# Moving the zero halves, x's other halves, addresses and lists of places among the table chunks, with column copying from step 3

## The chip, the core and the metric

The kernel runs on one core of one Trainium2 chip. The metric is the device time of one execution, in microseconds. Before the change the median of three runs is 2145.4 us (2143.6 to 2152.13).

The core's engines are PE (matrix products), DVE and ACT (element-wise work on the 128-partition memory, products' results included), POOL (here: it issues the gathers) and SP (here: it issues transfers). Each runs its own instructions in the order in which they are written, and they meet by semaphores. Transfers that SP and ACT issue share eight landing counters; each transfer is given one of them, and it is not issued before the last transfer of that counter has landed.

## What is computed

One layer of message passing on a graph: 12,500 nodes of 64 numbers (x), 200,000 edges with 32 numbers each (edge_attr), each edge with a source and a destination; the edges are sorted by destination.

```python
def _mlp(x, W1, b1, W2, b2):
    return relu(x @ W1 + b1) @ W2 + b2
msg_in = concatenate([nodes[row], nodes[col], edge_features], axis=-1)   # 64 + 64 + 32
messages = _mlp(msg_in, mW1, mb1, mW2, mb2)                              # 160 -> 128 -> 64
aggregated = segment_sum(messages, col, num_segments=12500)
upd_in = concatenate([nodes, aggregated], axis=-1)
out = layernorm(nodes + _mlp(upd_in, uW1, ub1, uW2, ub2))                # 128 -> 128 -> 64
```

Here row is the source of an edge and col its destination.

## The kernel before

**Tiles and steps.** The edges are cut into 1563 tiles of 128. A step works on six tiles (SUB), a group on two steps (twelve tiles, SUP); there are 261 steps. The first matrix of the message MLP is split by its three inputs. A = x times its rows for the source and B = x times its rows for the destination plus the bias are tables of one row per node. The hidden row h of an edge is the relu of A[source] + B[destination] + its edge numbers times the last rows.

**One step.** PE makes "pc" for six tiles: L410 multiplies an operand l (one-hot places of the destinations in a window of 32 rows, and the edge numbers) with rhs (a window of B and the weights of the edge numbers). Then the A rows come in: POOL gathers them, one instruction for each tile of 128 edges (L239), into nine row buffers, and PE adds them by a product with the identity (L437). DVE makes h from it by a relu (L450). In the next step L490 sums h over the destinations. The operand l and the selection band of a later group are made on DVE (L273, L281). SP loads what l and rhs need (L257 the destinations, L294 the edge numbers, L318 the window of B).

**The first eight steps** do not gather rows of A but rows of x itself (48 gathers, 64 numbers a row), since the table is not there yet. PE transposes them (L326) into PSUM "pt", ACT copies that to xt (L327), PE multiplies xt with the weights w1a (L429), and ACT makes h (L431). Gathers from table A begin at step 8 and wait until the whole table is written.

**The table chunks.** Ahead of step 0 table A is made in 13 chunks of eight blocks of 128 nodes (the last has two). A chunk is 16 or fewer matmuls into PSUM "pb" (L646), a copy of one half on ACT (L656), a copy of the other on DVE (L654), and one write of 512 KB that ACT issues (L658). pb has two buffers, and the copies' tile "tb" has four. The loop stands at L738 to L762: behind chunk k it issues four of the x gathers on POOL, the first of which waits for the chunk's ACT copy (eight more were issued ahead of the loop). Behind chunk 2 comes the first piece of table B, behind chunks 5 and 7 the operands of groups 0 and 1, and behind chunk 10 offsets(), a run of small DVE instructions on one partition that makes the lists of places from the list of windows.

**Column copying.** Not every A row is gathered. x transposed lies in the on-chip memory as xtop and xbot: blocks of nodes alternate between the two, and where one holds a node's 64 numbers the other holds zeros. For a copied group, its last two tiles (of six in the step) are not gathered from A. Each of the 128 columns of a tile "xc" is made instead from one column of xtop and one of xbot: ACT adds them (L381), DVE joins their bits (L389), each after loading the columns' addresses from col_a into registers (L357). PE then multiplies xc with w1a (L413). progress(s) says how many groups are to be copied by the end of step s; PACE gives its slope, and a group is used three steps later. COPIED lists the steps that use one: 118 of them, the first in steps 16, 18, 20.

**What the first steps do besides.** rest(s) issues the preparations of column copying: others() loads the other halves of xtop and xbot on SP (L630, L631, L633) in steps 3, 5 and 7; zeros() writes the zero halves on ACT (L639), two instructions of 64 x 1568 in each of the steps 3 to 10; columns_list() loads the source numbers (L336) and makes col_a on DVE (L339) in step 9. relative(), in steps 1 to 3, loads the destinations (L599) and the windows (L600, into col_a as scratch space) and subtracts them on DVE (L601).

**The order** of each engine is that of the program text, loop by loop (manual scheduling). Where a step gathers for a later one, its gathers are spread behind PE's matmuls by an added dependency called "pace".

Of the kernel before, what the change touches and what calls it, by code (L numbers as in the profile page):

```python
# [17 lines left out]
P = 128  # L18
# [56 lines left out]
LEAD = 8  # L75
SBASE = (33556480, 33554432)
CBASE = 33566720
PACE = ((11, 0.48), (50, 0.505), (130, 0.483), (170, 0.469), (261, 0))
# [49 lines left out]
def gnn_kernel(ctx: ExitStack, tc: tile.TileContext, x1T, x, eT, e_rows, src, src_row, dst, dst_row, wlist, wrow, wnext, whalf,  # L128
# [117 lines left out]
    with tc.tile_pool(name="work", bufs=2) as work, tc.manual_schedule():  # L246
# [74 lines left out]
        def transpose(s):  # L321

            a = xg.pop(s)[1]
            xt = work.tile([P, SUB // 2, P], F32, name="xt", tag="tb", bufs=4)
# [270 lines left out]

        def relative(a, b):

            wbc = col_a.rearrange("p a e b -> p (a e b)")[:, :b - a]
            nc.sync.dma_start(dst_s[:, a:b], dst[:, a:b])  # L599
            nc.sync.dma_start(wbc, wrow[:, a:b].broadcast_to([P, b - a]))  # L600
            nc.vector.tensor_tensor(drc[:, a:b], dst_s[:, a:b], wbc, op=ALU.subtract)  # L601
# [67 lines left out]
        def offsets():  # L669
# [5 lines left out]
            while k < K:  # L675
# [11 lines left out]
                k += n  # L687
            nc.vector.tensor_tensor(ustep[:, 1:], usup[:, 1:], usup[:, :-1], op=ALU.subtract)
            for v in (woff[:, :NSUB * LS], ustep[:, 1:]):
                nc.vector.tensor_scalar(v, v, 0.0, float(UN), op0=ALU.max, op1=ALU.min)  # L690
            v = woff[:, :NSUB * LS]
            nc.vector.tensor_scalar(wcnt[:, :NSUB * LS], v, 4.0, float(CBASE), op0=ALU.mult, op1=ALU.add)
            nc.vector.tensor_scalar(v, v, 4.0, float(SBASE[0]), op0=ALU.mult, op1=ALU.add)
            for k, d, n in runs:
                if k % 2 == 0:
                    k, n = k + 1, n - 1
                if n > 0:
                    o = ov[:, UPD[k]:UPD[k] + n * d].rearrange("o (n d) t -> o n (d t)", n=n)[:, ::2]
                    nc.vector.tensor_scalar(o, o, float(SBASE[1] - SBASE[0]), None, op0=ALU.add)

# [34 lines left out]
        for r in rhs:  # L735
            for o in EK:
                nc.sync.dma_start(r[o:o + DE], mW1[2 * D:, :].unsqueeze(1).broadcast_to([DE, SUP // 2, DH]))
        for k, c in enumerate(range(0, NB, NCH)):  # L738
# [4 lines left out]
            if k == 2:  # L743
                chunk_b(0, [B0v, Bv])
            if k == 3:
# [15 lines left out]
            if k == 10:  # L761
                offsets()  # L762
        assert not first

        def rest(s):

            if 3 <= s < 9 and s % 2:
                others((s - 3) // 2 * 4, (s - 3) // 2 * 4 + 4)
            if 3 <= s < 11:
                zeros(s - 3, 8)  # L770
            if s == 6:
                first_nodes(8, NODES)
            if s == 9:
                columns_list()
# [361 lines left out]
```

## Time and profile before

| | before |
|---|---|
| median of three runs | 2145.4 us |
| the profiled execution | 2147.86 us |
| its span in the trace | 2146.1 us |
| gathers from x / from table A | 48 / 1279 |
| single columns on ACT / on DVE | 7872 / 7232 |
| first copy of a chunk on ACT (L656) | 12.49 us |
| last copy of a chunk on ACT | 80.54 us |
| h of steps 0, 1, 2, 3 (start of L431) | 83.6, 87.3, 99.7, 112.1 us |
| first gather from table A | 84.58 us |

Times within the execution count from the start of the span. In a row of the timeline stand the start, the duration, the engine, the line of the kernel, the operation, what it writes and reads, its shape, and in brackets how long the engine had been idle before it and what released it. "remote" is a release that no recorded end explains, and "issue" is a time in which the engine waited for nothing that the profile shows. In a group of instructions stand the busy time of all, the mean of one in nanoseconds, and behind the second bar the idle time before them with its most frequent releaser. A busy share is an average over the whole span, so a stage of some ten microseconds doesn't show in it; for these the timeline and the table of stretches are read.

### The profile page before, as it was taken

How to read it: one execution, taken by the hardware profiler on the slowest of the kernel's cores; microseconds unless marked ns; L12 is line 12 of the kernel's file. 1: busy time of each engine (PE TensorE's matmuls, PEld its weight loads, DVE VectorE, ACT ScalarE, POOL GpSimd, SP SyncE). 2: the span in 40 equal slices, each digit the busy share in tenths (PEclk: the TensorE clock that was granted, in tenths of full speed). 3: DMA queues.
4: the chain of work that ended last, by engine and by line, in shares of the span. 5: the costliest groups of instructions: out<-in, count | busy, mean ns of one | idle time of the engine just before them, and what ended most of it. 6: DMA issues, size and time to landing. Idle time of an engine off the chain costs nothing. (4 is left out here: it accounts for less than half of the span.)

```text
span 2146.1 us, 47795 instructions
## 1 busy us (share of the span) xinstructions
PE 1692.0 (79%) x10742; PEld 1284.5 (60%) x10742; DVE 1135.8 (53%) x8047; ACT 1575.1 (73%) x8029; POOL 1257.7 (59%) x1336
## 2 busy tenths in 40 slices
PE   3476877888778887878887887888887888888888
PEld 3454665666555665656565656556665666666666
DVE  2414555565555555565555645565555565555553
ACT  1155988769869697889677877787877877878872
POOL 6565666665666666555656655565656666666650
PEclk8667877777787778787877777787788787878788
DMA  8452333332222222232223323233333333333331
GB/s 221 114 138 73 104 89 97 89 92 74 78 74 78 75 79 79 76 85 78 76 81 83 89 75 88 81 94 83 81 89 85 84 96 85 92 86 94 85 89 40
DMA packets 207836, 190.41 MB, mean 89 GB/s; under 512 B 57909, under 2 KB 174093, under 8 KB 207549
## 3 DMA queue, kind: packets, MB, share of 16 engines
q0 software_dynamic: 42464, 85.48, 16.0%
q1 hardware_dynamic: 150396, 92.86, 15.5%
q10 hardware_dynamic: 14690, 8.99, 1.5%
q8 instruction: 90, 1.47, 0.3%
q14 instruction: 196, 1.61, 0.2%
HBM read 169.15 MB, written 18.02 MB: 87 GB/s over the span
## 5 line engine op out<-in xcount | busy, mean ns | idle before, releaser
L239 POOL DMA_INDIRECT xg<-tab_a,src_s x1279 | 1211.0, 947 | 806.7 <-issue 264.7
L381 ACT ACTIVATE xc<-xtop,xbot 128x1 f32 x7872 | 1491.8, 293 | 163.6 <-issue 118.8
L389 DVE TENSOR_TENSOR xc<-xtop,xbot 128x1 int32 x7232 | 607.0, 155 | 470.6 <-issue 455.4
L490 PE MATMUL sums<-band,h 128*128 128x96 f32 x3126 | 539.2, 327 | 144.0 <-issue 88.4
L490 PEld LDWEIGHTS sums<-band,h 128*128 128x128 f32 x3126 | 476.8, 233 | 174.3 <-issue 103.4
L437 PE MATMUL pc<-xg,band 128*128 128x384 f32 (+1 forms) x1008 | 451.5, 574 | 31.8 <-issue 26.7
L410 PE MATMUL pc<-rhs,l 64*128 64x128 f32 x3126 | 371.5, 351 | 89.7 <-issue 66.3
L410 PEld LDWEIGHTS pc<-rhs,l 64*128 64x128 f32 x3126 | 291.8, 234 | 140.5 <-issue 97.5
L450 DVE TENSOR_SCALAR h<-pc 128x768 f32<-128x768 f32 x252 | 240.3, 953 | 197.2 <-PE sums L490 69.5
L437 PEld LDWEIGHTS pc<-xg,band 128*128 128x128 f32 x1008 | 216.4, 237 | 148.8 <-issue 96.3
L273 DVE TENSOR_TENSOR l<-l,cps 128x768 f32<-128x768 int32 (+1 forms) x134 | 127.1, 948 | 146.0 <-PE pc L437 66.8
L486 PEld LDWEIGHTS <-one 128*1 128x1 bf16 x1563 | 56.5, 81 | 215.3 <-issue 211.0
L561 ACT ACTIVATE y<-cps 128x256 f32<-128x256 f32 (+1 forms) x36 | 13.7, 382 | 179.8 <-issue 86.9
L486 PE MATMUL cnt<-band,one 128*1 128x32 bf16 x1563 | 89.6, 180 | 42.2 <-issue 40.9
L544 ACT ACTIVATE hTu<-sums,ub_s 128x416 f32<-128x416 f32 (+1 forms) x36 | 21.7, 603 | 96.0 <-PE pc L437 23.8
L413 PE MATMUL pc<-band,xc 64*128 64x128 f32 x472 | 77.6, 313 | 17.3 <-issue 16.7
L281 DVE TENSOR_TENSOR band<-cps,drc 128x384 f32<-128x384 f32 x131 | 71.7, 547 | 22.1 <-remote 14.9
L646 PE MATMUL pb<-band,xtop 64*128 64x128 f32 x200 | 43.7, 386 | 41.8 <-DVE tb L654 27.2
L413 PEld LDWEIGHTS pc<-band,xc 64*128 64x128 f32 x472 | 64.0, 228 | 15.5 <-issue 15.4
L646 PEld LDWEIGHTS pb<-band,xtop 64*128 64x128 f32 x200 | 38.3, 281 | 46.7 <-DVE tb L654 28.6
L239 POOL DMA_INDIRECT xg<-in_x,src_s x48 | 45.7, 952 | 24.3 <-issue 13.1
L552 PE MATMUL cps<-ux,xw 128*128 128x64 f32 x284 | 54.3, 347 | 5.2 <-issue 5.0
(107 smaller groups left out, 657.5 us busy)
## 6 DMA issues: line engine op xcount, KB each, us to landing
l<-in_dst_row SPq DMA_DIRECT2D x262, 96.0 KB
l<-in_eT SPq DMA_DIRECT2D x262, 96.0 KB
xg<-tab_a,src_s POOLq DMA_INDIRECT x1279
rhs<-tab_b SPq DMA_DIRECT2D x361, 32.0 KB
tab_b<-tb SPq DMA_DIRECT2D x13, 512.0 KB
rhs<-tab_b SPq DMA_DIRECT2D x387, 16.0 KB
tab_a<-tb ACTq DMA_DIRECT2D x12, 512.0 KB
out<-y SPq DMA_DIRECT2D x35, 128.0 KB
```

The lines of the kernel that those rows point to most:

```text
L239: ins = nc.gpsimd.indirect_dma_start(out=a[:, i, :] if s < XG else a[:, i // 2, i % 2, :], out_offset=None, in_=A[:, :] if s >= XG else x[ ...
L273: nc.vector.tensor_tensor(l[r], l[r].bitcast(I32), node[r].unsqueeze(2).broadcast_to([r.stop - r.start, SUP // 2, P]), op=ALU.is_equal)
L281: nc.vector.tensor_tensor(s[:, :nt], slot.unsqueeze(1).broadcast_to([P, nt, WIN]), drc[:, g * SUP:g * SUP + nt].unsqueeze(2).broadcast_to( ...
L381: nc.scalar.activation(o[:, e:e + 1], top.bitcast(F32), AF.Identity, bias=bot.bitcast(F32))
L389: nc.vector.tensor_tensor(o[:, e:e + 1].bitcast(I32), top.bitcast(I32), bot.bitcast(I32), op=ALU.bitwise_or)
L410: done = nc.tensor.matmul(pc[:, b, k, :], L[g][q:q + 64, m, :], rhs[g % 2][q:q + 64, w, :], start=k == 0, stop=False)
L413: done = nc.tensor.matmul(pc[:, b, k, :], xc[s][q:q + 64], w1a[q:q + 64], start=False, stop=False)
L437: added = nc.tensor.matmul(pc[:, b, :m], ident, a[:, b, :m], start=False, stop=True)
L450: nc.vector.tensor_scalar(h, pc, 0.0, None, op0=ALU.max)
L486: nc.tensor.matmul(pn8[:, bass.ds(cs[i] - CBASE, 4 * WIN)].bitcast(F32), one, SB[g][:, k0 + i, :, 1], start=False, stop=ends and i == n - 1)
L490: made.append(nc.tensor.matmul(ps8[:, bass.ds(ws[i] - SBASE[u % 2], 4 * WIDE * WIN)].bitcast(F32), h[:, i % 2, i // 2, :], widened(g, k0 + i),
L646: nc.tensor.matmul(pb[:, h, i, :], (xbot if h else xtop)[64 * h:64 * h + 64, (c + HB * h + i) * P:(c + HB * h + i + 1) * P], w[64 * h:64 * ...
```

## The change

Five things move or change.

- **Column copying starts at step 3**, not 11: the first number of PACE. 122 groups are copied, the first in steps 8, 10, 12. The gathers of their last two tiles go, and the copies of 128 columns each come in.
- **zeros()** is issued behind the chunks 0 to 7, not in steps 3 to 10.
- **others()** is issued behind the chunks 9, 10 and 11, not in steps 3, 5 and 7; SP's order has few instructions there, so they stand right behind the loads of group 1's edge numbers. **columns_list()** follows the chunks, ahead of step 0.
- **offsets()** yields between its instructions, and four of them at most follow each chunk from 5 on; what is left follows the last chunk.
- **Scratch space**: since col_a now holds addresses from the start, the windows for relative() go to hT, its loads stand in steps 1, 3 and 5 and its subtractions in steps 3, 5 and 7. xt goes to a buffer of the sums (sums_s) and no longer takes a "tb" tile.

```diff
--- before.py
+++ after.py
@@ -73,9 +73,10 @@
 U8 = mybir.dt.uint8
 YBASE = XBASE + 4 * XCOLS
 LEAD = 8
+OFFS = 4
 SBASE = (33556480, 33554432)
 CBASE = 33566720
-PACE = ((11, 0.48), (50, 0.505), (130, 0.483), (170, 0.469), (261, 0))
+PACE = ((3, 0.48), (50, 0.505), (130, 0.483), (170, 0.469), (261, 0))
 FINAL = 258
 
 
@@ -321,7 +322,7 @@
         def transpose(s):
 
             a = xg.pop(s)[1]
-            xt = work.tile([P, SUB // 2, P], F32, name="xt", tag="tb", bufs=4)
+            xt = sums_s[s % 2][:, :SUB // 2 * P].rearrange("p (k n) -> p k n", n=P)
             for k in range(SUB // 2):
                 nc.tensor.transpose(pt[:, k, :], a[:, 2 * k:2 * k + 2].rearrange("p k d -> p (k d)"), ident)
             nc.scalar.copy(xt, pt)
@@ -593,12 +594,15 @@
 
         WCH = 512
 
+        def absolute_load(a, b):
+
+            nc.sync.dma_start(dst_s[:, a:b], dst[:, a:b])
+            nc.sync.dma_start(hT.bitcast(I32)[:, :b - a], wrow[:, a:b].broadcast_to([P, b - a]))
+
         def relative(a, b):
 
-            wbc = col_a.rearrange("p a e b -> p (a e b)")[:, :b - a]
-            nc.sync.dma_start(dst_s[:, a:b], dst[:, a:b])
-            nc.sync.dma_start(wbc, wrow[:, a:b].broadcast_to([P, b - a]))
-            nc.vector.tensor_tensor(drc[:, a:b], dst_s[:, a:b], wbc, op=ALU.subtract)
+            nc.vector.tensor_tensor(drc[:, a:b], dst_s[:, a:b], hT.bitcast(I32)[:, :b - a],
+                                    op=ALU.subtract)
 
         def halves(a, b):
 
@@ -685,18 +689,25 @@
                                         op=ALU.subtract)
                 runs.append((k, d, n))
                 k += n
+                yield
             nc.vector.tensor_tensor(ustep[:, 1:], usup[:, 1:], usup[:, :-1], op=ALU.subtract)
+            yield
             for v in (woff[:, :NSUB * LS], ustep[:, 1:]):
                 nc.vector.tensor_scalar(v, v, 0.0, float(UN), op0=ALU.max, op1=ALU.min)
+                yield
             v = woff[:, :NSUB * LS]
             nc.vector.tensor_scalar(wcnt[:, :NSUB * LS], v, 4.0, float(CBASE), op0=ALU.mult, op1=ALU.add)
+            yield
             nc.vector.tensor_scalar(v, v, 4.0, float(SBASE[0]), op0=ALU.mult, op1=ALU.add)
+            yield
             for k, d, n in runs:
                 if k % 2 == 0:
                     k, n = k + 1, n - 1
                 if n > 0:
                     o = ov[:, UPD[k]:UPD[k] + n * d].rearrange("o (n d) t -> o n (d t)", n=n)[:, ::2]
                     nc.vector.tensor_scalar(o, o, float(SBASE[1] - SBASE[0]), None, op0=ALU.add)
+                    if k % 4 == 0:
+                        yield
 
         dst_s = drc.bitcast(I32)
         nc.scalar.dma_start(src_s[:, :64], src[:, :64])
@@ -735,6 +746,7 @@
         for r in rhs:
             for o in EK:
                 nc.sync.dma_start(r[o:o + DE], mW1[2 * D:, :].unsqueeze(1).broadcast_to([DE, SUP // 2, DH]))
+        places_made = offsets()
         for k, c in enumerate(range(0, NB, NCH)):
             copied = chunk_a(c)
             for i, u in enumerate(first[:EACH]):
@@ -742,6 +754,10 @@
             first = first[EACH:]
             if k == 2:
                 chunk_b(0, [B0v, Bv])
+            if k < 8:
+                zeros(k, 8)
+            if k > 8 and k < 12:
+                others((k - 9) * 4, (k - 9) * 4 + 4)
             if k == 3:
                 nc.vector.tensor_tensor(drc[:, :8 * SUP], dst_s[:, :8 * SUP], early, op=ALU.subtract)
                 first_nodes(0, 8)
@@ -758,24 +774,23 @@
                 load(g)
                 select(g)
                 counts(g)
-            if k == 10:
-                offsets()
+            if k > 4:
+                for _ in range(OFFS):
+                    next(places_made, None)
+        for _ in places_made:
+            pass
+        columns_list()
         assert not first
 
         def rest(s):
 
-            if 3 <= s < 9 and s % 2:
-                others((s - 3) // 2 * 4, (s - 3) // 2 * 4 + 4)
-            if 3 <= s < 11:
-                zeros(s - 3, 8)
             if s == 6:
                 first_nodes(8, NODES)
-            if s == 9:
-                columns_list()
-            if 1 <= s < 4:
-                relative(8 * SUP + (s - 1) * WCH, min(8 * SUP + s * WCH, NT))
-                if s == 2:
-                    halves(4 * SUP, NTP // 2)
+            for stage, a in ((relative, s - 3), (absolute_load, s - 1)):
+                if a in (0, 2, 4):
+                    stage(8 * SUP + a // 2 * WCH, min(8 * SUP + (a // 2 + 1) * WCH, NT))
+            if s == 2:
+                halves(4 * SUP, NTP // 2)
             if s == BS:
                 nc.sync.dma_start(wa, wrow.rearrange("o (p c) -> (o p) c", c=NSUP))
                 nc.sync.dma_start(wb, wnext.rearrange("o (p c) -> (o p) c", c=NSUP))
```

Lines of the changed kernel stand a few numbers further down than those of the kernel before (a copy on ACT is L656 there, L660 here).

The first place is in the table chunks. ACT's rows there for chunks 0 to 2, with the instructions' waits in brackets (the numbered DMAHW are the landing counters), before:

```order
L656 COPY tb_183<-pb_174 128x512 [waits PE_49]
L658 DMA tab_a_63<-tb_183 128x8x128 [waits DMAHW2_49,DVE_49]
L656 COPY tb_200<-pb_191 128x512 [waits PE_49]
L658 DMA tab_a_63<-tb_200 128x8x128 [waits DMAHW0_49,DVE_49]
L656 COPY tb_217<-pb_208 128x512 [waits PE_49]
```

and in the change, where two instructions of zeros stand behind each chunk's write, and chunk 1's write waits for the counter of chunk 0's (DMAHW2):

```order
L660 COPY tb_183<-pb_174 128x512 [waits PE_49]
L662 DMA tab_a_63<-tb_183 128x8x128 [waits DMAHW2_49,DVE_49]
L643 ACTIVATE xtop_66<-band_97 64x1568 [waits Pool_49]
L643 ACTIVATE xbot_67<-band_97 64x1568
L660 COPY tb_202<-pb_193 128x512 [waits PE_49]
L662 DMA tab_a_63<-tb_202 128x8x128 [waits DMAHW2_49,DVE_49]
L643 ACTIVATE xtop_66<-band_97 64x1568
L643 ACTIVATE xbot_67<-band_97 64x1568
L660 COPY tb_221<-pb_212 128x512 [waits PE_49]
```

In the same phase on DVE, its last copies of chunks; before, with the end of the lists of places ahead of chunk 11's copy (tb_441):

```order
L699 TENSOR_SCALAR lists_69<-lists_69 1x4x40
L699 TENSOR_SCALAR lists_69<-lists_69 1x6x32
L699 TENSOR_SCALAR lists_69<-lists_69 1x24
L654 COPY tb_441<-pb_432 128x512 [waits DMAHW3_49,Activation_49]
L273 TENSOR_TENSOR l2_82<-l2_82,cps_101 32x768 [waits DMAHW5_49]
```

and in the change, where the copies of chunks 10 and 11 (tb_446, tb_461) follow one another, with the addresses behind them:

```order
L708 TENSOR_SCALAR lists_69<-lists_69 1x6x32
L708 TENSOR_SCALAR lists_69<-lists_69 1x24
L658 COPY tb_446<-pb_437 128x512 [waits DMAHW4_49,Activation_49]
L658 COPY tb_461<-pb_452 128x512 [waits DMAHW7_49,Activation_49]
L340 TENSOR_SCALAR col_a_71<-cols_474 128x128 [waits DMAHW7_49]
```

The lists moved ahead of chunk 10's copy; nothing stands between the last two copies now.

The second place is SP behind the loads of group 1's edge numbers. Before:

```order
L294 DMA l1_81<-in_eT 32x768 [waits DMAHW2_49]
L310 TENSOR_LOAD lists_69
L318 ISA
L318 DMA rhs1_79<-tab_b0_65 64x1x128 [waits DMAHW4_49]
L257 DMA l2_82<-in_dst_row 32x6x128 [waits DMAHW5_49]
```

and in the change:

```order
L295 DMA l1_81<-in_eT 32x768
L634 DMA xtop_66<-in_x1T 64x4x512 [waits DMAHW2_49]
L635 DMA xbot_67<-in_x1T 64x4x512 [waits DMAHW3_49]
L634 DMA xtop_66<-in_x1T 64x4x512 [waits DMAHW5_49]
L635 DMA xbot_67<-in_x1T 64x4x512 [waits DMAHW6_49]
L634 DMA xtop_66<-in_x1T 64x4x512 [waits DMAHW0_49]
L635 DMA xbot_67<-in_x1T 64x4x512 [waits DMAHW1_49]
L637 DMA xbot_67<-in_x1T 64x256 [waits DMAHW3_49]
L337 DMA cols_474<-in_src_row 128x256 [waits DMAHW7_49,DMAHW4_49,DVE_49]
L337 DMA cols_474<-in_src_row 124x256 [waits DMAHW1_49]
L311 TENSOR_LOAD lists_69
```

Seven transfers of x's halves and two of source numbers now stand ahead of the loads for step 2.

The third place is ACT between the h of step 2 and that of step 3. Before:

```order
L431 ACTIVATE h_647<-pc_631 128x768 [waits PE_49,Activation_49]
L327 COPY xt_694<-pt_117 128x384 [waits PE_49]
L639 ACTIVATE xtop_66<-band_97 64x1568 [waits Pool_49]
L639 ACTIVATE xbot_67<-band_97 64x1568
L431 ACTIVATE h_727<-pc_699 128x768 [waits PE_49,Activation_49]
```

and in the change, its first rows (two more register loads with eight columns each follow before the next h):

```order
L432 ACTIVATE h_665<-pc_653 128x768 [waits PE_49,Activation_49]
L328 COPY sums_s0_73<-pt_117 128x384 [waits PE_49,Activation_49]
L358 TENSOR_LOAD col_a_71 [waits DMAHW3_49,DVE_49]
L382 ACTIVATE xc_706<-xtop_66,xbot_67 128x1 [waits DMAHW3_49,DMAHW1_49]
L382 ACTIVATE xc_706<-xtop_66,xbot_67 128x1 x7
L358 TENSOR_LOAD col_a_71
L382 ACTIVATE xc_706<-xtop_66,xbot_67 128x1 x8
```

Two instructions of zeros went, and 32 single columns with four register loads came.

## The prediction

> **What bounds the kernel now.** I read the busy time by engine first, then POOL's gathers by stretch, then the start row by row, and last what each engine waits for. The chain that ended last holds only the final norm and says nothing of the rest.
>
> The rows of the stretches give: stretch in us, its length, POOL's busy time (gathers in it), TensorE's granted clock, DMA share, GB/s.
>
> ```profile
> PE 1692.0 (79%) x10742; PEld 1284.5 (60%) x10742; DVE 1135.8 (53%) x8047; ACT 1575.1 (73%) x8029; POOL 1257.7 (59%) x1336
> 84.00:192.00 108.00, 69.03 (x73) 0.73 0.50 122
> 412.00:812.00 400.00, 243.59 (x258) 0.77 0.29 79
> 1212.00:1612.00 400.00, 237.53 (x251) 0.78 0.31 84
> 85.83 0.95 POOL L239 DMA_INDIRECT xg<-tab_a,src_s  x1 [0.30 <-issue]
> ```
>
> No engine is full. But a gather holds POOL for 0.95 + 0.30 = 1.25 us when it waits for nothing, so the 1327 gathers take 1659 us of the 2146: with its issue gaps POOL is about as full as any engine. In the middle a gather takes 400/258 = 1.55 to 400/251 = 1.59 us with its waits; between 84 and 192 us it is 108/73 = 1.48, nearer to the floor. The first steps, which gather all six tiles, lean on POOL harder than the rest.
>
> The second thing to see is how PE and POOL are tied. Here are chunk 11's last matmul, the copy that needs only it, and POOL's run of gathers meanwhile; then the same for the transposes of step 2:
>
> ```profile
> 64.11 0.34 PE L646 MATMUL pb<-band,xbot 64*128 64x128 f32 x1
> 57.02 0.95 POOL L239 DMA_INDIRECT xg<-in_x,src_s  x1 [3.83 <-ACT tb L656]
> 70.81 0.95 POOL L239 DMA_INDIRECT xg<-in_x,src_s  x1 [0.30 <-issue]
> 74.08 0.59 ACT L656 COPY tb<-pb 128x512 f32<-128x512 f32 x1 [8.69 <-remote]
> 89.79 0.49 PE L326 MATMUL pt<-band,xg 128*128 128x128 f32 x3
> 94.59 0.96 POOL L239 DMA_INDIRECT xg<-tab_a,src_s  x1 [0.30 <-issue]
> 97.42 0.48 ACT L327 COPY xt<-pt 128x384 f32<-128x384 f32 x1 [9.27 <-remote]
> 97.95 1.65 PE L429 MATMUL pc<-band,xt 64*128 64x128 f32 x12 [6.80 <-issue]
> POOL xg L239 <- remote: 172.6, 128, 2.6
> ```
>
> The matmul ends at 64.45 and its copy starts at 74.08; POOL's unbroken run of twelve gathers ended at 71.76. For the transposes it is 90.28, 97.42 and 95.55. So PE's word reaches the others about 2 us after a long run of gathers stops ("remote" is a release that fits no recorded end; POOL itself is held by such releases 128 times). A run of gathers costs the others its length, so I price a gather as time on the path. The Trainium skill, Perfetto Trace Analysis, Tensor Engine Instruction (MATMUL, LD_WEIGHTS), says that a matmul's recorded end is computed and that its semaphore rises only once PSUM has acknowledged the writes; by that rule the 9.6 us would be PE's own and not POOL's. It gives no length for the lag, and no row here has so long a lag while POOL rests.
>
> **The change part by part.** *The start.* A chunk of the tables is an ACT copy, a DVE copy and a write, and its x gathers wait for the ACT copy. The end of it:
>
> ```profile
> 65.42 0.69 DVE L654 COPY tb<-pb 128x512 f32<-128x512 f32 x1 [3.02 <-issue]
> 78.14 1.18 DVE L699 TENSOR_SCALAR lists<-lists 1x152 int32<-1x152 int32 x9
> 79.35 0.69 DVE L654 COPY tb<-pb 128x512 f32<-128x512 f32 x1
> 80.09 1.65 PE L410 MATMUL pc<-rhs,l 64*128 64x128 f32 x12 [12.75 <-DVE tb L654]
> ```
>
> The lists of places hold DVE from 66.05 to 79.32, and with it chunk 11's second copy, which could run at 74.08 + 0.59 = 74.67. The change cuts them into pieces that all stand before chunk 10's copy, so at best 79.35 - 74.67 = 4.7 us come free. Against that, ACT gets two zero halves in each of the chunks 0 to 7:
>
> ```profile
> L639 ACT ACTIVATE xbot<-band 64x1568 f32<-64x1568 f32 x8 | 12.1, 1510 | 0.1
> L639 ACT ACTIVATE xtop<-band 64x1568 f32<-64x1568 f32 x8 | 12.1, 1508 | 0.2
> 21.91 0.59 ACT L656 COPY tb<-pb 128x512 f32<-128x512 f32 x1 [1.18 <-DVE tb L654]
> 24.96 0.51 SPq L257 DMA_DIRECT2D l<-in_dst_row  x1
> 57.97 0.59 ACT L656 COPY tb<-pb 128x512 f32<-128x512 f32 x1 [1.22 <-DVE tb L654]
> ```
>
> That is 1.51 + 1.51 = 3.0 us a chunk, 24.2 in all. Their cover is ACT's idle time before most copies (14.4 us before chunk 7's, say). Where chunks follow at once (2, 4, 5, 6, 8) it is gone and the copy comes up to 3 us later. Chunk 1's write adds a wait: in the change it takes the landing counter of chunk 0's write. SP's load at 24.96 took that counter in the kernel before, so chunk 0's write had landed by then, and ACT may stand from 21.5 to 25.0 there. Behind it are the zeros and chunk 2's copy, now near 28 instead of 21.91, and POOL, which has gathers until 25.7 and then waits. Each pause of POOL so far cost 2.7 to 3.8 us from one gather's end to the next start (30.70 to 33.39, 53.18 to 57.02). I count one pause more than before, 3.2 us, against the 4.7: a start earlier by 1.5 us. Bounds: 4.7 earlier if no pause is added, 3 us later if two and a half are.
>
> *Others and the columns' list.* Six transfers of 512 KB and a small one, 3.2 MB by their shapes, go onto SP's queue behind the loads of step 2's edges, near 42 us. Columns as above but with PE, PEld, DVE, ACT and POOL; the last number is GB/s.
>
> ```profile
> 40.00:45.00 5.00, 2.08 (x16) 1.79 (x16) 0.70 (x2) 0.59 (x1) 3.78 (x5) 0.54 0.90 273
> 45.00:50.00 5.00, 0.00 (x0) 0.00 (x0) 0.00 (x0) 0.00 (x0) 3.78 (x5) 0.50 0.60 141
> 50.00:55.00 5.00, 0.00 (x0) 0.00 (x0) 0.00 (x0) 0.00 (x0) 2.57 (x3) 0.50 0.15 26
> 55.00:60.00 5.00, 2.08 (x16) 1.78 (x16) 3.16 (x5) 1.17 (x2) 2.37 (x3) 0.50 0.31 94
> ```
>
> At 273 GB/s these 20 us hold 5.5 MB and carry 2.7 (5 us of each rate), so 2.8 of the 3.2 MB fit and the rest is through by 62, before chunk 8's write waits for the first of them. I take nothing. Without this room it would be 3.2 MB / 273 GB/s = 12 us. The loads of rows and windows that stood before them on SP are needed from step 2 on, some 25 us later. The Trainium skill, DMA: Bandwidth & Descriptors, Queues, rings and completion order, speaks against the move: the DMA engines alternate between the queues, so a table write on ACT's queue would get half the rate while these run. By it a 512 KB write at half of 273 GB/s takes 3.8 instead of 1.9 us, and if two such writes gate copies the start gives back another 3.8 us. No row here shows these two streams together.
>
> *The steps.* Zeros leave ACT in steps 3 to 10, and 0.48 groups a step of column copies come in from step 3:
>
> ```profile
> 112.08 0.81 ACT L431 ACTIVATE h<-pc 128x768 f32<-128x768 f32 x1 [8.13 <-remote]
> 145.13 0.79 ACT L431 ACTIVATE h<-pc 128x768 f32<-128x768 f32 x1
> L381 ACT ACTIVATE xc<-xtop,xbot 128x1 f32 x208 | 38.9, 308 | 29.2 <-DMA ub_s<-in_ub 29.1
> 100.00:125.00 25.00, 19.96 (x142) 16.79 (x142) 2.97 (x5) 9.51 (x10) 16.32 (x19) 0.64 0.57 138
> 125.00:150.00 25.00, 17.44 (x126) 14.67 (x126) 1.51 (x2) 13.35 (x12) 16.04 (x17) 0.64 0.59 134
> ```
>
> Steps 3 to 7 take (145.13 - 112.08)/4 = 8.3 us. A group is 7872/118 = 67 single columns on ACT, so a step gets 32, at 38.9/208 = 0.187 us 6.0 us, with h and xt (0.81 + 0.48) 7.3: under 8.3, so I take nothing. If h must wait behind the columns without cover it is 6.0 - 3.0 = 3 us more a step. DVE was nearly idle there (2.97 and 1.51 us of 25), so its share costs nothing either. Before, ACT stood from 158 to 187 and then worked off 208 columns in one run; that run held up nothing that waits show, so its end gives nothing.
>
> What counts is that four more of the groups up to step 20 leave two gathers each to the columns: 8 gathers of 73. At the middle's 1.55 us a gather the 65 left take 100.8 us instead of 108: 7.2 us less. Bounds: nothing if PE's own chain sets the step, and 8 x 1.48 = 11.8 if every gather is on the path. I take 7.2, since the middle runs this very mix. From step 21 on the number of groups per step is the same, only shifted by a step or two; nothing.
>
> *Small moves.* xt in sums_s frees buffers that nothing waited for (its wait at 97.42 was PE's word), hT for col_a likewise: nothing, none where the loads come two steps ahead.
>
> **Sum:** 1.5 + 7.2 = 8.7 us. From the profiled execution, 2147.86 us, that is 2139.2; it stands 2.5 above the median of the runs, 2145.4, so the forecast is 2136.7 us.
>
> **The rivals.** *More comes free*: no pause is added and every gather counts, and the late xt of step 2 comes with a shorter run of gathers: 4.7 + 11.8 = 16.5, so 2129 us. For it: 6.8 us of PE standing at 97.95. Against it: ACT's zeros stand in the path of chunk 8. *PE sets the step*: the late word is PE's own, fewer gathers only lengthen POOL's waits, and the start alone counts: 2144 us. For it: POOL waits for PE at every step; against it the step of 8.3 us with six gathers a step. *The chunks go at ACT's pace*, slower than before: when the zeros make POOL pause after every chunk from 3 to 9, each costs 4 x 1.25 + 3.2 = 8.2 us, 32.5 + 7 x 8.2 = 89.9 for what ended at 71.76, so 18.1 later, less 4.7 and 7.2: 2152 us. It decides as soon as a copy comes over 5.0 us after the one before (copy, write, zeros and DVE's wait are 0.59 + 0.37 + 3.0 + 1.22 = 5.2, so it is close); against it stands that several copies are ready at one pause, as at 56.16 and 57.97. *Columns ahead of h*: 3 us more in five steps eats the gathers' gain, 15 - 1.5 later, 2159 us; it decides where PE's word for h comes before the columns are through.
>
> **How the numbers follow.** Chances: forecast 0.40, more free 0.18, PE sets the step 0.20, ACT's pace 0.14, columns ahead 0.08. A change under 0.5% (10.7 us, 2134.7 to 2156.1) counts as none, about what this measurement can tell. The forecast's own range is 2131 to 2142, two fifths of it under 2134.7: 0.16, with the first rival 0.34, rounded up to 0.36 as both ends lean on POOL. Slower is the last rival, and half of ACT's pace, if its pauses are longer: 0.15. The rest, 0.49, is no change. The range takes in the first rival and ACT's pace: 2127 to 2153.
>
> **What would show it.** Right: chunk 11's second copy near 77 to 78 instead of 79.35, h of step 0 at about 82; 65 gathers from the first table gather to step 13, at over 1.5 us each; no DVE lists after chunk 10. Wrong: POOL idle over 3 us more than three times before 75 us, the others' transfers still running at 70, h of steps 4 to 7 starting right behind a column copy, or the same step length with more POOL idle.

## The result and the profile after

The changed kernel takes 2138.2 us in the median of 11 runs, the kernel before 2146.4 us in as many; the ratio is 0.9948, with a 95% interval of 0.9933 to 0.9962. The forecast was 2136.7 us. The profiled execution has a span of 2136.4 us, 9.7 less than the profile before.

The first page line of the changed kernel shows the busy time of its engines:

```profile
PE 1694.9 (79%) x10758; PEld 1285.1 (60%) x10758; DVE 1152.6 (54%) x8295; ACT 1618.9 (76%) x8293; POOL 1252.3 (59%) x1328
```

Eight gathers are gone from POOL, and ACT and DVE have the 264 and 248 single columns more. ACT's busy time grew by 44 us and the span shrank, so ACT is not what bounds the kernel on this chip.

The timeline of the changed kernel, from the table chunks to step 14 (ACT, with one row of POOL and one of DVE):

```profile
28.02 0.56 ACT L660 COPY tb<-pb 128x512 f32<-128x512 f32 x1
29.34 0.37 ACTq L662 DMA_DIRECT2D tab_a<-tb  x1
29.75 1.51 ACT L643 ACTIVATE xtop<-band 64x1568 f32<-64x1568 f32 x1 [1.17 <-issue]
31.27 1.51 ACT L643 ACTIVATE xbot<-band 64x1568 f32<-64x1568 f32 x1
32.69 0.56 ACT L660 COPY tb<-pb 128x512 f32<-128x512 f32 x1
...
69.54 0.59 ACT L660 COPY tb<-pb 128x512 f32<-128x512 f32 x1 [8.09 <-remote]
...
76.51 0.37 ACT L660 COPY tb<-pb 128x256 f32<-128x256 f32 x1 [1.22 <-PE pt L327]
76.91 0.46 ACTq L662 DMA_DIRECT2D tab_a<-tb  x1
...
79.64 0.81 ACT L432 ACTIVATE h<-pc 128x768 f32<-128x768 f32 x1 [1.75 <-PE pc L430]
...
83.48 0.95 POOL L240 DMA_INDIRECT xg<-tab_a,src_s  x1 [7.49 <-DMA l<-in_eT]
...
116.53 6.04 ACT L382 ACTIVATE xc<-xtop,xbot 128x1 f32 x32 [0.25 <-issue]
122.47 0.79 ACT L432 ACTIVATE h<-pc 128x768 f32<-128x768 f32 x1
...
200.60 0.95 DVE L451 TENSOR_SCALAR h<-pc 128x768 f32<-128x768 f32 x1
```

Four times are to be read here. Chunk 12's copy, the last, starts at 76.51 us (80.54 before), h of step 0 at 79.64 (83.63), the first gather from table A at 83.48 (84.58), and h of step 14 at 200.60 (210.4). So 4.0 us come from the start and another 5.8 from the steps up to 14, if the border is drawn at h of step 0; drawn at the first gather from table A, it is 1.1 and 8.7. The end of the span is 9.7 us earlier: in this pair of profiles the rest of the kernel neither gains nor loses.

Two stretches show the gathers from the first one out of table A to h of step 13, first of the changed kernel, then of the kernel before (stretch, its length, POOL's busy time and gathers, granted clock, DMA share, GB/s):

```profile
83.48:183.84 100.36, 63.21 (x67) 0.74 0.36 94
```

```profile
84.58:191.60 107.02, 68.63 (x73) 0.73 0.51 123
```

That is 1.50 us a gather after and 1.47 before. The rate is nearly the same and there are fewer of them.

### The profile page after: what moved, and what is told of

The parts are those of the page before. It is cut to its first block, busy times and chain, and to the rows that moved or that the text cites. A ratio compares the mean times of both kernels' runs of the same rounds, so it can differ in the third digit from the quotient of the medians.

```text
span 2136.4 us, 48405 instructions
## 1 busy us (share of the span) xinstructions
PE 1694.9 (79%) x10758; PEld 1285.1 (60%) x10758; DVE 1152.6 (54%) x8295; ACT 1618.9 (76%) x8293; POOL 1252.3 (59%) x1328
## 3 DMA queue, kind: packets, MB, share of 16 engines
q8 instruction: 90, 1.47, 0.3%
## 5 line engine op out<-in xcount | busy, mean ns | idle before, releaser
L382 ACT ACTIVATE xc<-xtop,xbot 128x1 f32 x8136 | 1536.8, 280 | 149.6 <-issue 106.1
L390 DVE TENSOR_TENSOR xc<-xtop,xbot 128x1 int32 x7480 | 625.7, 154 | 489.3 <-issue 474.0
L438 PE MATMUL pc<-xg,band 128*128 128x384 f32 (+1 forms) x1008 | 456.7, 580 | 39.6 <-issue 38.6
L555 PE MATMUL cps<-u2c,hTu 128*128 128x64 f32 x284 | 55.3, 347 | 7.6 <-issue 7.6
```

The source lines that it names most:

```text
L382: nc.scalar.activation(o[:, e:e + 1], top.bitcast(F32), AF.Identity, bias=bot.bitcast(F32))
L390: nc.vector.tensor_tensor(o[:, e:e + 1].bitcast(I32), top.bitcast(I32), bot.bitcast(I32), op=ALU.bitwise_or)
L438: added = nc.tensor.matmul(pc[:, b, :m], ident, a[:, b, :m], start=False, stop=True)
```

## The experiments

The experiments ran in three groups, each on one chip and beside runs of the kernel before on it. The chips were not alike: the kernel before took 2173.0 us in the first group, 2146.4 in the second and 1690.4 in the third. Ratios are taken within a group only, and the change itself did not run on the chips of the first and the third. This table has the stages of each profile, in us from the start of the span; "last copy" is chunk 12's, "gather" the first from table A, and the last column is the time from that gather to h of step 14. A stage is read from one execution, and that can lie some way from the median of its kernel (e1's 8.7 and e4's 8.8 us under it, e2's 4.6 over it), so what a kernel costs in all is read from the ratios.

| kernel | ratio to before (95%) | last copy | h of step 0 | gather | h of step 14 | from gather to h of step 14 |
|---|---|---|---|---|---|---|
| before, first profile | 1 | 80.5 | 83.6 | 84.6 | 210.4 | 125.8 |
| the change | 0.9948 (0.9933–0.9962) | 76.5 | 79.6 | 83.5 | 200.6 | 117.1 |
| group 1, chip of 2173.0 us | | | | | | |
| e1_start11 | 1.0001 (0.9991–1.0012) | 73.8 | 77.0 | 80.4 | 205.8 | 125.4 |
| e2_lists_block | 0.9998 (0.9987–1.0010) | 85.9 | 88.9 | 89.8 | 207.5 | 117.8 |
| e3_gathers_out | 0.9946 (0.9932–0.9959) | 74.1 | 77.3 | 80.6 | 195.7 | 115.0 |
| e4_columns_only | 1.0017 (1.0005–1.0028) | 75.0 | 78.1 | 82.2 | 209.9 | 127.7 |
| group 2, chip of 2146.4 us | | | | | | |
| c_before | 1.0008 (0.9993–1.0023) | 87.1 | 90.2 | 91.1 | 216.4 | 125.2 |
| c_change | 0.9949 (0.9929–0.9969) | 76.7 | 79.9 | 83.8 | 200.8 | 116.9 |
| l1_lists_only | 0.9961 (0.9945–0.9977) | 69.1 | 74.4 | 74.9 | 200.8 | 126.0 |
| v1_addresses_later | 0.9946 (0.9927–0.9965) | 77.3 | 80.4 | 85.4 | 201.1 | 115.7 |
| group 3, chip of 1690.4 us | | | | | | |
| b1_lists_zeros | 1.0046 (1.0031–1.0061) | 68.4 | 71.6 | 74.4 | 158.0 | 83.6 |
| b2_lists_halves | 1.0006 (0.9997–1.0016) | 63.3 | 67.2 | 69.5 | 139.3 | 69.7 |
| e1r_start11 | 1.0052 (1.0036–1.0067) | 68.0 | 71.1 | 73.7 | 141.9 | 68.2 |
| d1_zeros_in_gaps | 1.0113 (1.0096–1.0131) | 73.9 | 76.9 | 79.2 | 168.9 | 89.6 |

### Column copying from step 11 again

```diff
-PACE = ((3, 0.48), (50, 0.505), ...
+PACE = ((11, 0.48), (50, 0.505), ...
```

> The change with column copying from step 11 again (118 groups); zeros, x's other halves, addresses and lists stay among the chunks. Theory of the prediction (a start of its own plus eight gathers on the path): h of step 0 as in the change, near 79.6 us, but the steps after it as slow as before: h of step 14 near 79.6 + (210.4 - 83.6) = 206.4 us, and some 6 us more than the change in all, about 2144 us. Rival, that the steps became faster because the zeros and the 3.2 MB of x's halves left them: h of step 14 near 200.6 as in the change, 2138 us.

Measured: from h of step 0 to h of step 14 it takes 205.8 - 77.0 = 128.8 us, where the change took 121.0 and the kernel before 126.8, both on a chip that is 1.2% faster in all; from the first gather it is 125.4, against 117.1 and 125.8. So the steps are as slow as before although the zeros and x's halves have left them; the rival falls. The whole is 1.0001 of before: what was moved among the chunks, the lists with the rest, brings nothing in sum on this chip.

### The gathers out, and the columns alone

Both take the four groups of steps 8, 10, 12 and 14 apart: e3 drops their gathers and makes no columns, e4 makes the columns and keeps the gathers.

```diff
+LEFT = COPIED + [8, 10, 12, 14]      # e3, on e1
+LEFT = COPIED[4:]                    # e4, on the change
...
-            return tiles(s)[:SUB - 2 * (s in COPIED)]
+            return tiles(s)[:SUB - 2 * (s in LEFT)]
...
-                copied = s in COPIED and i >= SUB - 2      # e4 alone
+                copied = s in LEFT and i >= SUB - 2
...
-                    m = SUB // 2 - (s in COPIED)
+                    m = SUB // 2 - (s in LEFT)
```

> As e1_start11, but the last two gathers of steps 8, 10, 12 and 14 are left out with nothing in their place (the source part of those eight tiles is missing), so eight gathers fewer without the columns. Theory: h of step 14 near 200.6 us as in the change, 2138 us; the gathers alone bring the 6 us over e1_start11. If columns on ACT hold h up (h of step 5 began right behind its columns in the change), it is earlier still, by 2 to 4 us. Rival, PE sets the step: as e1_start11, 206.4 us.

> The change with the columns of the first four groups (steps 8, 10, 12, 14) made, but their gathers kept and the columns not used: the columns' cost without the gathers' gain. Theory (columns hide): as e1_start11, h of step 14 near 206.4 us, about 2144 us. Rival, columns ahead of h: later than e1_start11 by up to 3 us a step in steps 3 to 7, h of step 14 at 210 to 218 us.

The rows of h of steps 0 and 14, of e1, then of e3:

```profile
76.96 0.81 ACT L432 ACTIVATE h<-pc 128x768 f32<-128x768 f32 x1 [1.75 <-PE pc L430]
...
205.83 0.95 DVE L451 TENSOR_SCALAR h<-pc 128x768 f32<-128x768 f32 x1
```

```profile
77.30 0.81 ACT L433 ACTIVATE h<-pc 128x768 f32<-128x768 f32 x1 [1.75 <-PE pc L431]
...
195.69 0.95 DVE L452 TENSOR_SCALAR h<-pc 128x768 f32<-128x768 f32 x1
```

The stretches from h of step 0 to h of step 14 of e1, e3 and e4 (busy us of PE, PE's weight loads, DVE, ACT and POOL, then granted clock, DMA share and GB/s):

```profile
76.96:205.83 128.87, 85.21 (x569) 64.34 (x571) 34.57 (x146) 32.72 (x139) 75.31 (x80) 0.70 0.33 87
```

```profile
77.30:195.69 118.39, 80.91 (x575) 62.70 (x577) 34.68 (x146) 32.56 (x139) 67.93 (x72) 0.74 0.34 90
```

```profile
78.11:209.87 131.76, 97.51 (x569) 74.18 (x571) 54.70 (x387) 78.54 (x380) 75.60 (x80) 0.62 0.32 87
```

Eight gathers less shorten this stretch from 128.9 to 118.4 us, by 10.5; that is 1.3 us a gather. The ratios say 0.55% of 2173, or 12 us. PE loses with them the products of eight tiles, and its busy time falls by 4.3 us; even if all of that were on the path, it would leave 6.2 of the 10.5, so "PE sets the step" falls on this chip. The columns alone (e4) make the stretch 209.9 - 78.1 = 131.8 us, 2.9 more than e1's, and the whole 0.16% longer, some 3.5 us; the two intervals overlap, so this cost is only likely. In that profile the granted clock was 0.62 in this stretch and 0.70 in e1's, and PE took 12.3 us longer for the same number of products, so the 2.9 us may be the clock's and not the columns'. Gathers and columns together come to 10.5 - 2.9 = 7.6 us.

The last column of the table bears this out over two chips. With the gathers of all six tiles it is 125.2 to 126.0 us (before twice, e1, l1), with eight gathers replaced by columns 115.7 to 117.8 (the change twice, e2, v1), with the gathers dropped 115.0 (e3) and with columns added to them 127.7 (e4). Eight gathers replaced are worth some 7 to 10 us on the way from the first gather to h of step 14.

### The lists of places

```diff
-            if k > 4:
-                for _ in range(OFFS):
-                    next(places_made, None)
+            if k == 10:
+                for _ in places_made:
+                    pass
```

> The change with the lists of places in one run behind chunk 10, as before. Theory (the run held chunk 11's copy on DVE): h of step 0 goes back from 79.6 to about 83.6 us and everything behind it with it, but the first gather from table A moves less than h, since it waits for the last table writes; 2138 + 2 to 4 us. Rival, that h of step 0 came earlier because of when POOL's gathers run: h of step 0 stays under 81 us.

On the same subject l1 has the pieces of the change and nothing else of it, and the kernel before was profiled a second time:

```diff
-            if k == 10:
-                offsets()
+            if k > 4:
+                for _ in range(OFFS):
+                    next(places_made, None)
```

> The kernel before with the lists of places cut into pieces behind chunks 5 to 9, and nothing else of the change. If the lists' run on DVE is what the start waits for, chunk 12's copy and h of step 0 come up to 4.7 us earlier (h near 79 us); the time 0 to 4 us less than before. If the 13 us only fill a wait that POOL's run of gathers makes anyway, h of step 0 stays within 1.5 us of 83.6 and the time is that of before.

> The kernel before once more, for its stages in a second profile: h of step 0 at 83.6 us, of step 14 at 210.4, and a ratio of 1 by all theories; what it differs from the first profile is what a single profile can't tell.

> The changed kernel once more, beside the others of this call on one chip, since e1 to e4 ran on a chip whose kernel before took 2173 us and the change was timed where it took 2146. If the change brings the same there as here: 0.9948 of the kernel before. If it depends on the chip, it is within 0.2% of e1_start11's 1.0001.

The second profile of the kernel before, from chunk 10's copy to h of step 0:

```profile
72.90 0.59 ACT L656 COPY tb<-pb 128x512 f32<-128x512 f32 x1 [11.37 <-remote]
...
84.67 1.18 DVE L699 TENSOR_SCALAR lists<-lists 1x152 int32<-1x152 int32 x9
85.88 0.69 DVE L654 COPY tb<-pb 128x512 f32<-128x512 f32 x1
...
87.07 0.37 ACT L656 COPY tb<-pb 128x256 f32<-128x256 f32 x1 [11.83 <-DVE tb L654]
...
90.17 0.81 ACT L431 ACTIVATE h<-pc 128x768 f32<-128x768 f32 x1 [1.75 <-PE pc L429]
```

and l1 with the lists in pieces:

```profile
69.14 0.37 ACT L657 COPY tb<-pb 128x256 f32<-128x256 f32 x1 [1.22 <-PE pt L327]
...
74.39 0.81 ACT L432 ACTIVATE h<-pc 128x768 f32<-128x768 f32 x1 [3.87 <-PE pt L327]
...
74.88 0.95 POOL L240 DMA_INDIRECT xg<-tab_a,src_s  x1 [1.77 <-issue]
...
200.84 0.95 DVE L451 TENSOR_SCALAR h<-pc 128x768 f32<-128x768 f32 x1
```

The lists run between chunk 10's second copy and chunk 11's, for 13.3 us in the first profile and 11.7 in the second. In the first, chunk 10's copy came at 64.80, and a late word of PE's covered most of the run (the word is the rise of the semaphore by which PE tells that a matmul is done; here chunk 11's copy waited for it until 74.08). In the second profile chunk 10's own copy came only at 72.90, after 11.37 us of waiting. Its last matmul had ended at 64.38, so this was the late word too, but ahead of the run and not beside it; little covered the run, and h of step 0 came at 90.2 instead of 83.6.

l1's h of step 0, at 74.4, is 9.2 us ahead of the one profile and 15.8 of the other, not 4.7. Not all of this is the run on DVE: in l1 the late word is missing as well. Chunk 11's last matmul ended at 65.66, its word came at 65.68 in the midst of a run of gathers, and its copy started at 67.34, not at 74.08. Whether the pieces made the word come in time or it happened so, these profiles can't say, nor how often which comes. By the runs the pieces alone are worth 0.39%, 8 us. In e2 chunk 12's copy goes back to 85.9 and h of step 0 to 88.9, more than the 83.6 that was expected. e2's whole time is that of the kernel before; what it loses to the change can't be given, since the change did not run on that chip.

### The addresses later

```diff
-        columns_list()
         assert not first
...
+            if s == 0:
+                columns_list()
```

> The change with the addresses (columns_list) made in step 0, so that SP's loads for step 2 no longer stand behind a load that waits for chunk 9's tile (SP stood from 59.8 to 74.8 us in the change). If those loads slow the last two table writes (5.8 and 6.3 us from issue to landing, 3.2 and 2.8 before), the loads go at 60 us, the first gather from table A comes near 80.5 instead of 83.5 us and the time is 0 to 3 us under the change. If the contention counts for nothing, the same time as the change and the first gather within 1 us of 83.5.

These rows are of the changed kernel, SP's issues around its stand, and the row that groups its wait (what waited for what, us in total, times, longest):

```profile
59.77 0.63 SPq L637 DMA_DIRECT2D xbot<-in_x1T  x1
74.81 1.23 SPq L337 DMA_DIRECT2D cols<-in_src_row  x2
77.39 0.76 SPq L319 DMA_DIRECT2D rhs<-tab_b  x1
78.21 1.88 SPq L258 DMA_DIRECT2D l<-in_dst_row  x2
80.13 2.56 SPq L295 DMA_DIRECT2D l<-in_eT  x2
```

```profile
SPq L337 <- DMA tab_a<-tb: 13.7, 1, 13.7
```

The load of the source numbers goes into a "tb" tile, which is free when a table write has landed, so SP stood and the loads for step 2 ran against the last two writes. From the last write's issue to the first gather it took 83.48 - 76.91 = 6.6 us, and 84.58 - 80.94 = 3.6 before: the start's 4.0 us became 1.1 at the gathers. (The gather's row names a load of l as its releaser; that load was given the landing counter of one of the two writes, and the last of the writes landed at 82.75.) v1 did not mend this. Its loads of destinations did go at 63.7, but the source numbers still stood until 75.6, in the same writes' way; the first gather came at 85.4 and the time is that of the change.

A run in which the last writes have no company is e2. There the lists hold them back until the source numbers and the first loads for step 2, issued from 75.1 to 78.9 us, have landed. Its last write and first gather:

```profile
86.26 0.37 ACTq L662 DMA_DIRECT2D tab_a<-tb  x1
...
89.78 0.94 POOL L240 DMA_INDIRECT xg<-tab_a,src_s  x1 [14.21 <-DMA tab_a<-tb]
```

That is 3.5 us, as in the kernel before. In e1, on the same chip and with the loads beside the writes, it is 80.41 - 74.19 = 6.2. So the loads beside them cost these writes some 3 us. What that is worth in the whole time no run shows.

### Zeros and x's halves one by one

```diff
+            if k < 8:                                      # b1, on l1
+                zeros(k, 8)
+            if k > 8 and k < 12:                           # b2, on l1
+                others((k - 9) * 4, (k - 9) * 4 + 4)
...
-            if 3 <= s < 11:                                # b1
-                zeros(s - 3, 8)
...
-            if 3 <= s < 9 and s % 2:                       # b2
-                others((s - 3) // 2 * 4, (s - 3) // 2 * 4 + 4)
```

> l1_lists_only with the zero halves behind chunks 0 to 7 in addition (x's other halves, addresses and columns as in the kernel before). l1's chunks ended with a copy at 69.1 us, h of step 0 at 74.4; the change's at 76.5 and 79.6. If ACT's zeros are what the change gave back, this run has the chunk copies of the change (spaced 4.7 us from 28 us on), the last near 76 and h of step 0 near 79.5 us, and 3 to 6 us more than l1. If not, h of step 0 stays near 74.4 and it is x's halves on SP.

> l1_lists_only with x's other halves loaded behind chunks 9 to 11 in addition (zeros, addresses and columns as before). If the transfers hide, chunk copies and h of step 0 as in l1 (69.1 and 74.4 us) and the first gather from table A within 1 us of 74.9; if they take rate from the table writes, the last writes take over 4 us and the first gather comes 1.5 us or more later.

> e1_start11 again, on the chip of this call. From stages: h of step 0 as in the change near 79.7, steps as before, h of step 14 near 206.3 us; beside l1's 0.9961 (h of step 14 200.8) that is 5 to 6 us more, 0.998 to 0.999. On the slower chip it was 1.0001.

These three and the next ran on the fast chip, so l1's times do not hold for them; they are compared with each other. Where the zeros stand among the chunks the last copy starts at 68.4 us (b1) and 68.0 (e1r), where they stand in the steps at 63.3 (b2): 5 us, and 4 at h of step 0. e1r and b2 both have x's halves among the chunks and differ by the zeros and the addresses, which come behind the copies. The spacing of copies in b1 is 4.7 us from 28 to 47 us, as expected of it. So the zeros cost the start about 5 us on this chip. In the second group the change's h of step 0 (79.9) is 5.5 behind l1's (74.4), but a late word of PE's at chunk 9 stands between these two as well (8.09 us of waiting ahead of its copy, in both profiles of the change). Whether x's halves slow the writes stays open: from the last write to the first gather it is 5.6 us in b1 and 5.8 in b2. In b1, which has them in the steps, PE stood once, in step 6, for a window of B that SP loads behind them (issued at 91.58, behind two of the halves at 88.36 and 89.04):

```profile
99.27 1.65 PE L411 MATMUL pc<-rhs,l 64*128 64x128 f32 x12 [6.39 <-DMA rhs<-tab_b]
```

Its h of step 14 comes at 158.0 us, e1r's at 141.9, and yet both take the same time in the end (medians of 1698.0 and 1697.8 us): 16 us at the start do not show in the time on this chip. The order of the totals is another there, too. b1 is 0.46% slower than before, and e1r 0.52%, where the same kernel was equal to before in the first group.

### Zeros in the gaps

```diff
-            if k < 8:
-                zeros(k, 8)
+        make_identity(nc, ident)                          # from a few lines further down
...
+        zeros(0, 8)                                       # ahead of chunk 0
...
+            for i in {0: (1, 2), 2: (3, 4), 4: (5,), 5: (6, 7)}.get(k, ()):
+                zeros(i, 8)
...
-            cols = work.tile([P, 2, 2, P], I32, name="cols", tag="tb", bufs=4)
+            cols = hT.bitcast(I32).rearrange("p (r b e) -> p r b e", r=2, b=2)
```

> The change with its zeros in ACT's gaps (one ahead of chunk 0, two behind chunk 0, two behind chunk 2, one behind 4, two behind 5) and the source numbers loaded into hT, so that SP waits for no table tile. If zeros in the copies' path and SP's wait are what the change gave back: chunk 12's copy near 70, h of step 0 near 75, the first gather near 76 us in place of 83.5, and the steps of the change behind it: h of step 14 near 75 + 121 = 196 us, 4 to 6 us under the change (ratio to before near 0.992). If the gain at the start is lost again in the steps: the change's 0.995.

Neither part of this came. Chunk 0's write stood on ACT from 13.6 to 22.4 us, until a load of x had landed, with four instructions of zeros behind it, and chunk 1's copy came at 28.85; the gap was not where it had been. And the whole is 1.13% slower than before on this chip, 0.6% slower than e1r. Where the time may go is seen in the group of the columns on ACT, of e1r and of d1 (duration of one in ns, then first and last start in us):

```profile
L382 ACT ACTIVATE xc<-xtop,xbot x7872: 277/292/318, 122.9 to 1641.8; 128x1 f32 x197
```

```profile
L382 ACT ACTIVATE xc<-xtop,xbot x8136: 277/288/393, 92.9 to 1663.1; 128x1 f32 x199
```

and in one stretch in the middle, of e1r and then of the kernel before on the first chip (busy us of PE, PEld, DVE, ACT and POOL):

```profile
500.00:900.00 400.00, 318.59 (x2428) 250.12 (x2435) 274.37 (x2120) 400.00 (x2148) 302.46 (x321) 0.88 0.36 100
```

```profile
500.00:900.00 400.00, 319.91 (x1944) 239.36 (x1943) 220.54 (x1703) 333.00 (x1757) 243.65 (x258) 0.78 0.29 76
```

In e1r, on the fast chip, ACT is busy 400 of 400 us in this stretch. POOL is as full: it starts a gather every 400/321 = 1.25 us, the 0.95 + 0.30 of one that waits for nothing. Which of the two bounds the kernel there is not separated. d1's columns begin 30.0 us earlier than e1r's, but the 264 columns more take (1663.1 - 92.9) - (1641.8 - 122.9) = 51.3 us more, so they end 21.3 later; the span is 14.5 us longer. That the columns are the cause is argued from this and not shown: d1 differs from e1r in its zeros and loads too, and neither the change nor the columns alone were run on this chip.

## Why the prediction was right, and which of its steps were not

**The time and its sign** came as forecast: 8.7 us less were predicted and the medians differ by 8.2. That the number is so close is luck. By the ratios the lists in pieces are worth 8 us (l1). The lists and all else that moved among the chunks are worth nothing together (e1), so zeros, x's halves and addresses take about as much as the lists bring. The gathers and columns bring 12 - 3.5 = 8.5 us (e3 and e4). The forecast had 4.7, 3.2 and 7.2 for the three. This is an estimate across two chips, and each term may be off by 3 us or so. On its own chip the change (0.9949) and l1 (0.9961) can't be told apart, so cutting the lists and doing nothing else would have brought most of the gain.

**A gather as time on the path: right on the chips of 2146 and 2173 us.** 7.2 us were predicted for the steps; the change's steps to 14 are 126.8 - 121.0 = 5.8 us shorter in the first pair of profiles and 126.2 - 120.9 = 5.3 in the second, and 8.7 and 8.3 if counted from the first gather. Of its two parts, the gathers alone bring 10.5 (e3), close to the bound of 11.8, and the columns perhaps take some 3 back (e4), where the prediction had them hidden on ACT. In the change h of step 5 starts at 122.47, right behind 32 columns that began at 116.53; this was named as a sign against it. 67 gathers ran from the first to h of step 13, where 65 were forecast.

**The step that failed is the start, "one pause more than before, 3.2 us, against the 4.7".** h of step 0 was predicted 1.5 us earlier and was 4.0 in the first pair and 10.3 in the second; chunk 11's second copy came at 75.32, where 77 to 78 was named. The last x gather ends 4.2 us later than before (75.99 and 71.76), but not by one pause: POOL's waits between the x gathers grew by 1.8 us, and two gathers took 1.85 and 2.46 us in place of 0.95. They ran beside the lists' long instructions on DVE, one of them here:

```profile
63.49 2.46 POOL L240 DMA_INDIRECT xg<-in_x,src_s  x1 [0.30 <-issue]
64.59 1.24 DVE L699 TENSOR_SCALAR lists<-lists 1x2088 int32<-1x2088 int32 x1
```

The same is seen in the change's second profile (2.45 and 1.85) and in l1 (1.48, 1.86 and 1.69); before, these instructions ran when POOL had no gather left. And h of step 0 does not wait for the last x gather but for chunk 12's copy, 3.1 us behind it in both kernels. The price of the lists of places was read off one execution in which a late word of PE's covered most of their run; l1 shows what they are worth alone: most of the whole gain. What was priced too low on the other side are the zeros. "The chunks go at ACT's pace" was a rival with 5.2 us a chunk; the spacing measured is 4.7 where chunks follow at once, just under the 5.0 us of four gathers, so POOL seldom starves, but the last copy comes at 76.5 instead of l1's 69.1. Not all of that is the zeros: chunk 9's copy waited for PE's word (65.13 to 69.54), and the last lists still hold chunk 10's second copy from 71.88 to 73.52.

**Others and the columns' list: nothing was taken, and that was wrong by about 3 us at the first gather.** The room on the DMA engines was there, the free tile was not: SP stood until 74.8 us, and the table writes had company. The Trainium skill, DMA: Bandwidth & Descriptors, Queues, rings and completion order, has the DMA engines alternate between queues; the 6.6 us in place of 3.6, and e1's 6.2 beside e2's 3.5, agree with it, for the loads of step 2 and not for x's halves, which were through.

**PE's late word** was the reading on which the price of a gather rested. In e1r, on the fast chip, it is gone. POOL's gathers, the transposes of step 3 and their copy:

```profile
78.71 0.94 POOL L240 DMA_INDIRECT xg<-tab_a,src_s  x1 [0.30 <-issue]
...
79.95 0.95 POOL L240 DMA_INDIRECT xg<-tab_a,src_s  x1 [0.30 <-issue]
...
80.34 0.49 PE L327 MATMUL pt<-band,xg 128*128 128x128 f32 x3
...
80.92 0.48 ACT L328 COPY sums_s<-pt 128x384 f32<-128x384 f32 x1 [1.25 <-PE pt L327]
...
81.20 0.94 POOL L240 DMA_INDIRECT xg<-tab_a,src_s  x1 [0.30 <-issue]
```

The copy follows the last transpose (80.83) by 0.1 us in the midst of a run of gathers; on the first chip it was 7.1. By the Trainium skill, Perfetto Trace Analysis, Tensor Engine Instruction (MATMUL, LD_WEIGHTS), the semaphore rises only after PSUM has acknowledged; at 0.1 us that part is small here, so unless it differs from chip to chip it is not what makes the lag of the first one.

The traces also record the rises of PE's semaphore themselves. In the kernel before, on the first chip, a rise follows the computed end of its matmul within 0.08 us in 155 of 302 cases while POOL gathers nothing, and in 2 of 89 when a run of gathers has lasted over 5 us; in e1r, on the fast chip, it does so in 1762 of 1959 of the latter. So on the first chip the lag goes with runs of gathers, as the prediction had it, though not in every run (l1's chunk 11 above) and not by a fixed 2 us behind its end (in the second profile of the kernel before the run ended at 69.62 and chunk 10's copy started at 72.90). Why one chip has it and another has not stays open.

## What to carry to other kernels

A run of small instructions that one engine does for later use is cut into pieces before anything larger is moved: it can cost its whole length when the waits beside it happen to fall elsewhere, and one profile may show it half hidden. Work that is moved into an engine's gaps is priced by what stands behind it in the queue, a write that waits for a landing counter among it, not by the gap's length. And a price per instruction holds for the bound it was read from: where gathers delay the others a copied column is worth it, and where ACT is full, as on the fast chip, it may cost its own time.

## What the runs showed of the hardware

The same kernel took 2146.4, 2173.0 and 1690.4 us on three chips. On the fast one the granted clock is 0.88 to 0.89 in the runs of the kernel before, on the two others 0.77 to 0.79. PE's word is seldom late there: in the middle of e1r a gather starts every 1.25 us, against 400/258 = 1.55 for the kernel before on the first chip. How much of the difference is the clock's and how much the late word's was not measured. Which kernel is faster changes with the chip: the edit of e1 is equal to before on one and 0.5% slower on another.

On the first chip a gather that took 0.95 us alone took 1.48 to 2.46 us beside DVE instructions on 1x2088 numbers, in the change and in l1.
